# Two windowed transformers on one core: which operand of P times V stays in the array, and where P is divided by its sums

## The chip, the core and the metric

The kernel runs on one core of a Trainium2 chip. Its time is the device time of one execution in microseconds (us); three runs gave a median of 3963.43 us (3961.78 to 3975.84). TensorE is PE in the profile (its weight loads are PEld), VectorE is DVE, ScalarE is ACT, GpSimd is POOL, and SP issues most of the DMAs.

## The reference, cut to what matters

The reference is a chain of four blocks, each a product of an attention and a gated feed-forward net added to x. The change touches two of the feed-forward nets, which are themselves small transformers with attention in a window: "l2" (6 layers, 16 heads, window W = 32, run on 4 sequences of 512 tokens) and "l3" (2 layers, 8 heads, window 64). All is fp32, heads have 64 values. One layer's attention is

```
q = l2norm(q) * qs ; k = l2norm(k) * ksc          # then rotary tables
sim  = einsum('bhwie,bhwje->bhwij', q, k) * 8     # 2W keys for W queries
attn = softmax(where(mask, -max, sim), -1)
out  = einsum('bhwij,bhwje->bhwie', attn, v)
x    = x + out.reshape(b, n, INNER) @ Wo          # then the feed-forward layer
```

A query block of W tokens sees its own block of keys and the one before it, so P (the softmax before the division) has 2W columns for each query and head.

## The kernel before, in words

Both transformers are one class, `_Transformer`. The flag `split` is true for l2 and false for l3. Three generators run interleaved: `queries_keys` (projections, squares, norms, rotary tables, L1268 to L1330), `attention` (L1476 to L1521) and `feed_forward`. Each yields an estimate of the PE time that it has just issued, and `merge` always continues the one that is furthest behind its share; `attention_weight` (L1199) is attention's share. A round of the three is called a slot here: l2 has 48 slots of work (6 layers, 4 sequences, 2 groups of 8 heads), l3 has 8. The order in which an engine then runs its instructions is fixed when the program is built, and it isn't quite the order of the code: in the trace some work stands ahead of work that was written before it.

Attention works in units: 96 in l2 and 32 in l3. A unit is half of a group's heads for 128 T tokens (T = 4 in l2, 2 in l3). In the loop over units, pass i does this:

- `scores` (from L1370) for unit i: a mask goes into two PSUM banks by an identity matmul, then small matmuls (L1389) add the scores, 64 of them in l2 (64 rows by 32 columns of the array each, 64 columns moving) and 16 in l3 (64 by 64, 128 moving). In the middle of them it calls `turn` for unit i-1. After them DVE takes the maxima (L1399), subtracts them (L1403), ACT takes exp (L1408), DVE sums (`rs`, L1410) and inverts the sums (`r`, L1412).
- `turn` (from L1415): 8 PE transposes of P, by `Net.transpose` (L126), and one ACT copy to SBUF (`PT`, L1424).
- `turn_back` (from L1465) for unit i-2: PE transposes of `On` (8 in l2, 4 in l3, again L126) and two ACT copies into `OT` (L1474). After the second unit of a pair come four matmuls of `OT` with `Wo` (by `Net.mm`, L122) and the addition to y (L1513).
- `weigh` (from L1427) for unit i-1: P times V. The turned P is the weight that is loaded, and V moves: 64 matmuls in l2, each 64 rows by 32 columns with 64 columns of V moving, and 16 in l3, each 128 rows by 64 columns with 64 moving. DVE then multiplies by r on the way out of PSUM into `On` (L1454 in l2, L1459 in l3).
- `values` for a later unit: V by matmuls, an ACT copy (L1352) and DMAs.

Each fp32 matmul of the code stands twice in the trace as a weight load and a MATMUL: the 6,144 small matmuls of `weigh` in l2 are 12,288 MATMULs. Transposes stand once.

All PSUM tiles of a transformer come from one pool of four tiles of two banks (`S2`, `M`). On POOL, `queries_keys` puts the sum of two squares (L1294) and the rotary addition (L1298); SP carries the DMAs of Q, K, V and the weights. `part` (L1222 to L1238) loads a weight when it is first asked for; `Wo` has three buffers.

Of the kernel before, what the change touches and what calls it, by code (L numbers as in the profile page):

```python
# [16 lines left out]
F32 = mybir.dt.float32  # L17
# [1153 lines left out]
class _Transformer:  # L1171
    def __init__(self, net, pre, heads, window, pools, consts):
        self.net, self.nc, self.a, self.pre = net, net.nc, net.a, pre
        self.heads, self.W, self.inner = heads, window, heads * 64
        self.GP = heads // 8
        self.NB = 128 // window
        self.split = self.NB == 4
        self.PS, C, self.TB, self.WT, self.QK, self.VP, self.PP, self.TP = pools
        nc, a = self.nc, self.a
        self.T = 4 if self.split else 2  # L1180
        self.NU = self.T * 64 // window
        self.cols = net.load(C, a[pre + "cols"], name=pre + "_cols")
        k = net.load(C, a[consts][:, 0:256], name=pre + "_k", queue=nc.scalar)
        self.ones, self.cen = k[:, 0:128], k[:, 128:256]
        self.tiny = C.tile([128, 1], F32, name=pre + "_tiny")
        nc.vector.memset(self.tiny, 1e-36)
        n = NT // self.T
        self.mask = C.tile([128, n, 512], BF16, name=pre + "_mask")
        nc.gpsimd.dma_start(self.mask, a[consts][:, 256 : 256 + 512 * n].rearrange("p (t n) -> p t n", t=n))
        self.identb = C.tile([128, 128], BF16, name=pre + "_identb")  # L1190
        nc.vector.tensor_copy(self.identb, net.ident)

        self.ve = [C.tile([128, self.NU, 1024 // self.NB], F32, name=f"{pre}_ve{i}") for i in range(2)]
        for i in range(2 if self.split else 1):
            for lo, hi in self.second():
                nc.gpsimd.memset(self.ve[i][lo:hi, 0, :], 0.0)
        self.made, self.shift, self.weights = {}, {}, {}

        self.attention_weight = 20.4 if self.split else 25.0  # L1199
        self.feed_forward_weights = (7.7, 1.7) if self.GP == 2 else (9.4,)  # L1200


        self.lag = 1 if self.split else 0
        self.y = net.xn
# [17 lines left out]
    def part(self, kind, l, gp):  # L1222

        key = kind, l, gp
        if key not in self.weights:
            nc, a, pre = self.nc, self.a, self.pre
            if kind == "qk":
                t = self.WT.tile([128, 1024], F32, name=pre + "_wqk", bufs=2)
                nc.sync.dma_start(t, a[pre + "Wqkv"][l][:, 1024 * gp : 1024 * (gp + 1)])
            elif kind == "v":  # L1230
                t = self.WT.tile([128, 512], F32, name=pre + "_wv", bufs=2)
                c = 2 * self.inner + 512 * gp
                nc.sync.dma_start(t, a[pre + "Wqkv"][l][:, c : c + 512])
            else:
                t = self.WT.tile([128, 4, 128], F32, name=pre + "_wo", bufs=3)
                nc.sync.dma_start(t, a[pre + "Wo"][l][512 * gp : 512 * (gp + 1)].rearrange("(t p) n -> p t n", p=128))
            self.weights[key] = t
        return self.weights[key]  # L1238

# [130 lines left out]
    def scores(self, qk, tp, j, last):  # L1370
# [39 lines left out]
        nc.vector.tensor_reduce(rs, P.rearrange("p t g e k -> p (t g e) k"), axis=AX.X, op=ALU.add)  # L1410
        r = net.stat(n, "r")
        nc.vector.reciprocal(r, rs)  # L1412
        return P, r

    def turn(self, u):  # L1415

# [7 lines left out]
        self.nc.scalar.copy(u["PT"], t)  # L1424
        yield 0.9

    def weigh(self, u):  # L1427

        net, nc, W, T = self.net, self.nc, self.W, self.T
        PT, r, vo, ve, tp, j = (u[k] for k in ("PT", "r", "vo", "ve", "tp", "j"))  # L1430
        On = self.PP.tile([128, 2 * T, 2, 64], F32, name=self.pre + "_On", bufs=1)
        o = self.S2() if self.split else self.M()
        for i in range(2 * T):
            g = i % 2
            for bl in range(self.NB):
                c = self.NB * (T * tp + i // 2) + bl
                v, k = (vo if c % 2 else ve), c // 2 - tp * self.NU
                for e in range(2):
                    if self.split:
                        rows, d = slice(64 * e, 64 * e + 64), 64 * (2 * g + j)  # L1440
                        net.mm(
                            o[W * bl : W * bl + W, e, 64 * i : 64 * i + 64], PT[rows, i, W * bl : W * bl + W],
                            v[rows, k, d : d + 64],
                        )
                    else:
                        n, d = 2 * i + e, 64 * (4 * g + 2 * j + e)
                        net.mm(
                            o[W * bl : W * bl + W, 64 * n : 64 * n + 64], PT[:, n, W * bl : W * bl + W], v[:, k, d : d + 64]
                        )
            yield 0.3 if self.split else 0.15  # L1450
        rv = r.rearrange("p (n e) -> p n e", e=2)
        if self.split:
            for e in range(2):
                nc.vector.tensor_tensor(  # L1454
                    On[:, :, e, :], o[:, e, :].rearrange("p (n d) -> p n d", d=64),
                    rv[:, :, e].unsqueeze(2).to_broadcast([128, 2 * T, 64]), ALU.mult,
                )
        else:
            nc.vector.tensor_tensor(  # L1459
                On.rearrange("p n e d -> p (n e) d"), o.rearrange("p (n d) -> p n d", d=64),  # L1460
                r.unsqueeze(2).to_broadcast([128, 4 * T, 64]), ALU.mult,
            )
        u["On"] = On

    def turn_back(self, u, OT):  # L1465

        net, T = self.net, self.T
        t = (self.S2() if self.split else self.M().unsqueeze(1)).rearrange("p a (b q) -> p (a b) q", q=128)
        for i in range(2 * T):
            net.transpose(t[:, i, :], u["On"][:, i].rearrange("p e d -> p (e d)"))  # L1470
        ov = OT.rearrange("p (g j) (t q) -> p j g t q", j=2, t=T)
        tv = t.rearrange("p (t g) q -> p g t q", g=2)
        for g in range(2):
            self.nc.scalar.copy(ov[:, u["j"], g], tv[:, g])  # L1474

    def attention(self, rows):  # L1476

        net, nc, T = self.net, self.nc, self.T  # L1480
        n = NT // T
        units = [dict(l=l, b=b, gp=gp, tp=tp, j=j) for l, b in rows for gp in range(self.GP) for tp in range(n) for j in range(2)]
        of_slot = len(units) // len(rows) // self.GP
        for piece in self.values(units[0]):
            if piece:
                yield piece
        for i in range(len(units) + 2):
            if i > self.lag and i % of_slot == self.lag or i == 1 and self.lag:
                yield None
            u = units[i] if i < len(units) else None  # L1490
            last = units[i - 1] if 0 < i <= len(units) else None
            older = units[i - 2] if i > 1 else None
            if u:
                if i % of_slot == 0:
                    qk = self.made.pop((u["l"], u["b"], u["gp"]))
                if u["j"] == 1:
                    u["ve"], u["vo"] = last["ve"], last["vo"]
                u["P"], u["r"] = yield from self.scores(qk, u["tp"], u["j"], last)
            elif last:
                yield from self.turn(last)  # L1500
            if older:
                if older["j"] == 0:
                    OT = self.TP.tile([128, 4, 128 * T], F32, name=self.pre + "_OT", bufs=1)
                self.turn_back(older, OT)
                yield 0.9 if self.split else 0.45
                if older["j"] == 1:
                    wo = self.part("o", older["l"], older["gp"])
                    p = self.M()[:, 0 : 128 * T]
                    for t in range(4):
                        net.mm(p, wo[:, t, :], OT[:, t, :], t == 0, t == 3)  # L1510
                        yield 0.86 if self.split else 0.43
                    ys = net.tok(self.y, older["b"])[:, 128 * T * older["tp"] : 128 * T * (older["tp"] + 1)]
                    nc.vector.tensor_tensor(ys, ys, p, ALU.add)  # L1513
                older.clear()
            if last:
                yield from self.weigh(last)
            if u and i + 2 < len(units) and u["j"] == 0:
                ahead = self.values(units[i + 2])
                yield from until_none(ahead)
            elif u and i + 1 < len(units):  # L1520
                yield from until_none(ahead)  # L1521
# [185 lines left out]
```

## Time and profile before

| what | value |
|---|---|
| median of 3 runs | 3963.43 us |
| the profiled execution's own time | 3955.01 us |
| its span (first to last instruction) | 3953.3 us |
| PE busy, whole span | 3577.5 us (90%) |
| DVE busy | 2452.6 us (62%) |
| ACT busy | 1845.0 us (47%) |
| POOL busy | 1157.9 us (29%) |
| l2, about 1650 to 3395 us of the span | 48 slots, 37.6 us each in the middle of a layer |
| l3, about 3540 to 3930 us | 8 slots, 51.85 us each in the middle |

The page of a profile gives busy shares over the whole span. Since the program is a row of different stages, the views for one stretch of time (windows, timeline, waits) are the ones to go by for a change that touches only two stages. A busy PE is a PE with some matmul in flight, so the spacing of the starts says more about its speed than the duration of one row.

### The profile page before, as it was taken

What the parts mean: (1) busy time and instruction counts of PE and PEld (TensorE: products, weight loads), DVE (VectorE), ACT (ScalarE), POOL (GpSimd) and SP (SyncE); (2) the same over time, 40 slices, a digit from 0 to 9 for tenths busy, and PEclk for the clock granted to TensorE, in tenths of its full rate; (3) what the DMA queues carried; (4) which work ended last, traced back from release to release, by engine and by line L of the source; (5) the groups of instructions that cost most, each with busy time, mean ns of one, the idle gap of its engine ahead of it and who ended that gap; (6) DMA issues with size and microseconds to landing.
All of it is one profiled execution on the core that took longest, in us unless ns stands there. A gap on an engine that the chain in (4) does not pass through costs nothing.

```text
span 3953.3 us, 105287 instructions
## 1 busy us (share of the span) xinstructions
PE 3577.5 (90%) x46763; PEld 1880.3 (48%) x46891; DVE 2452.6 (62%) x3429; ACT 1845.0 (47%) x2510; POOL 1157.9 (29%) x994
## 2 busy tenths in 40 slices
PE   7786999899999998889999999999999999778887
PEld 4553455444444443444444554554444445445554
DVE  6674555413353341677777787777777777457774
ACT  3343666523133324454555554555455455535555
POOL 1000444300021112533334343343443343033220
PEclk7677999999699999999999999999999999889998
DMA  1000000001000001434344434334334333413221
GB/s 38 8 26 28 1 1 1 30 0 51 2 1 3 3 1 37 106 86 115 88 96 110 98 91 109 95 91 119 93 83 117 86 80 94 130 37 83 54 56 42
DMA packets 123574, 236.12 MB, mean 60 GB/s; under 512 B 29624, under 2 KB 44128, under 8 KB 117728
## 3 DMA queue, kind: packets, MB, share of 16 engines
q1 hardware_dynamic: 114064, 209.58, 21.7%
q10 hardware_dynamic: 8624, 19.29, 1.5%
q8 instruction: 369, 6.05, 0.6%
q0 software_dynamic: 432, 0.51, 0.1%
q14 instruction: 85, 0.70, 0.1%
HBM read 50.08 MB, written 5.54 MB: 14 GB/s over the span
## 4 chain that ended last, share of the span: by engine, by line
PE 62%; DVE 13%; ACT 12%; issue 6%; DMA 3%; POOL 2%; SPq 1%; DVEq 0%; ACTq 0%; POOLq 0%
PE S L122 39%; PE S L126 5%; PE M L122 5%; PE S L1389 4%; PE o L1094 3%; ACT l_P L581 3%; PE o L614 2%; DVE l_rot L1295 2%; DVE rotp L1297 1%; DMA l_tab<-in_k_rot_l 1%; DVE l_rot L1321 1%; PE S L1008 1%; ACT sqp L1293 1%; ACT l_PT L1424 1%; SPq L1328 1%
## 5 line engine op out<-in xcount | busy, mean ns | idle before, releaser
L1298 POOL TENSOR_TENSOR l_rot<-l_rot,rotp 128x1024 f32<-128x1024 f32 x224 | 528.6, 2362 | 324.7 <-DVE rotp L1297 313.3
L1294 POOL TENSOR_TENSOR sqp<-sqp 128x512 f32<-128x512 f32 x224 | 291.5, 1301 | 956.6 <-ACT sqp L1293 952.0
L122 PE MATMUL S<-hb,l_wqk 128*128 128x512 f32 x896 | 476.8, 622 | 38.1 <-ACT l_PT L1424 10.7
L1293 ACT ACTIVATE sqp<-S 128x1024 f32<-128x1024 f32 x224 | 230.2, 1027 | 305.1 <-PE S L122 304.1
L1321 DVE SCALAR_TENSOR_TENSOR l_rot<-S,l_rot 128x1024 f32<-128x1024 f32 x224 | 264.6, 1219 | 133.8 <-ACT S L1318 110.6
L126 PE MATMUL S<-core,l_P 128*128 128x128 f32 x1856 | 266.9, 288 | 40.1 <-ACT l_P L1408 17.3
L122 PE MATMUL S<-l_KT,l_QT 32*128 32x256 f32 (+7 forms) x1536 | 264.2, 510 | 34.7 <-ACT l_P L1116 14.5
L1295 DVE TENSOR_TENSOR l_rot<-S,l_tab 128x1024 f32<-128x1024 f32 x224 | 271.2, 1211 | 24.6 <-ACT sqp L1293 24.0
L1389 PEld LDWEIGHTS S<-l_qk 64*32 64x32 f32 (+1 forms) x13312 | 178.5, 108 | 217.7 <-issue 211.2
L1116 ACT ACTIVATE l_P<-S 128x1024 f32<-128x1024 f32 x160 | 156.7, 1022 | 252.3 <-PE S L122 251.7
L126 PEld LDWEIGHTS S<-core,l_P 128*128 128x128 f32 x1856 | 213.3, 146 | 128.1 <-issue 39.3
L1297 DVE TENSOR_TENSOR rotp<-S,l_tab 128x1024 f32<-128x1024 f32 x224 | 270.8, 1209 | 1.4 <-POOL l_rot L1298 1.3
L1389 PE MATMUL S<-l_qk 64*32 64x64 f32 (+1 forms) x13312 | 249.5, 230 | 18.8 <-DMA l_qk<-l_rot 1.7
L122 PE MATMUL S<-sqp,l_k 128*128 128x512 f32 x448 | 251.9, 648 | 13.4 <-POOL sqp L1294 6.6
L122 PE MATMUL S<-l_wv,hb 128*64 128x256 f32 (+1 forms) x1600 | 237.2, 400 | 5.5 <-DVE rotp L1297 4.2
L1069 DVE TENSOR_REDUCE l_mx<-S 128x2 f32<-128x768 f32 (+1 forms) x192 | 155.0, 864 | 136.7 <-PE S L1008 136.7
L122 PEld LDWEIGHTS S<-l_ve,l_PT 64*32 64x32 f32 (+1 forms) x6656 | 164.3, 108 | 152.5 <-issue 124.9
L1399 DVE TENSOR_REDUCE mx<-S 128x16 f32<-128x1024 f32 (+1 forms) x128 | 156.3, 1221 | 116.1 <-PE S L1389 112.2
L122 PEld LDWEIGHTS S<-hb,l_wqk 128*128 128x128 f32 x896 | 147.2, 191 | 168.6 <-issue 92.0
L122 PE MATMUL S<-l_OT,l_wo 128*128 128x512 f32 (+1 forms) x512 | 218.9, 543 | 8.3 <-DVE ffu L1551 7.9
L1120 POOL TENSOR_SCALAR_AFFINE_SELECT l_P<-l_P 128x256 f32<-128x256 f32 x256 | 99.4, 406 | 417.0 <-ACT l_P L1116 411.6
L1317 ACT ACTIVATE S<-S,l_tiny 128x1024 f32<-128x1024 f32 x112 | 121.9, 1089 | 198.4 <-PE S L122 180.2
(358 smaller groups left out, 6580.1 us busy)
## 6 DMA issues: line engine op xcount, KB each, us to landing
l_qk<-l_rot SPq DMA_DIRECT2D x896, 128.0 KB
l_ve<-l_vo SPq DMA_DIRECT2D x112, 256.0 KB
l_ve<-l_vo SPq DMA_DIRECT2D x96, 224.0 KB
l_tab<-in_k_rot_l ACTq DMA_DIRECT2D x16, 1024.0 KB
l_wqk<-in_l2Wqkv SPq DMA_DIRECT2D x12, 512.0 KB
l_wv<-in_l2Wqkv SPq DMA_DIRECT2D x12, 256.0 KB
l_wo<-in_l2Wo SPq DMA_DIRECT2D x12, 256.0 KB
l_ve<-l_vo SPq DMA_DIRECT2D x24, 128.0 KB
```

The lines of the kernel that those rows point to most:

```text
L122: self.nc.tensor.matmul(out, lhsT, rhs, start=start, stop=stop)
L126: self.nc.tensor.transpose(out, in_, self.ident[:n, :n])
L1069: nc.vector.tensor_reduce(mxv[:, bs, 2 * m + e, 3 - i], s[u][:, :, c : c + n], axis=AX.X, op=ALU.max)
L1116: nc.scalar.activation(P[u], s[u], AF.Exp, scale=scale)
L1293: nc.scalar.activation(sq, p, AF.Square)
L1294: nc.gpsimd.tensor_tensor(sq[:, 0, :], sq[:, 0, :], sq[:, 1, :], ALU.add)
L1295: nc.vector.tensor_tensor(t[:, g], p, tab[:, 0], ALU.mult)
L1297: nc.vector.tensor_tensor(m, p, tab[:, 1], ALU.mult)
L1298: nc.gpsimd.tensor_tensor(t[:, g], t[:, g], m[:, ::-1, :], ALU.add)
L1321: nc.vector.scalar_tensor_tensor(t[:, g], p[:, g, :].unsqueeze(1).to_broadcast([128, 2, S]), 1e12, t[:, g], ALU.min, ALU.mult)
L1389: net.nc.tensor.matmul(sv[W * bl : W * bl + W, e, t, g, :].rearrange("p (s k) -> p s k", s=2), qk[0][r, g, j, W * c : W * c + W], kw, star ...
L1399: nc.vector.tensor_reduce(mx, flat, axis=AX.X, op=ALU.max)
```

## The change

- In `weigh` the two operands change places: 64 columns of V are the weight that is loaded, and the turned P moves (32 columns in l2, 64 in l3). O comes out with its 64 values on partitions and tokens along the free axis, as `Wo` needs it, so ACT copies it straight into `OT`; `turn_back` with its transposes is gone, and so is `On`.
- In l2 the matmuls alternate over four quadrants of 64 by 64 of the array: head e reads rows 64e, and the block's parity s sends it to columns 64 (e xor s) and to PSUM bank s. Heads stand the other way round for odd blocks, so `Wo` is kept twice, the second time with its halves exchanged (two more DMAs for each load, two buffers instead of three), and the four `Wo` matmuls of 512 columns become eight of 256.
- r can no longer be multiplied onto O, whose queries are along the free axis now. P is divided by its sums before it is turned: one POOL multiplication of 128 by 1024 for each unit, in place.
- In l3 the shape of the `weigh` matmuls stays (128 rows by 64 columns, 64 moving).

```diff
-        self.attention_weight = 20.4 if self.split else 25.0
+        self.attention_weight = 18.6 if self.split else 23.0
...
-                t = self.WT.tile([128, 4, 128], F32, name=pre + "_wo", bufs=3)
-                nc.sync.dma_start(t, a[pre + "Wo"][l][512 * gp : 512 * (gp + 1)].rearrange("(t p) n -> p t n", p=128))
+                t = self.WT.tile([128, 2 if self.split else 1, 4, 128], F32, name=pre + "_wo", bufs=2)
+                wo = a[pre + "Wo"][l][512 * gp : 512 * (gp + 1)].rearrange("(t p) n -> p t n", p=128)
+                nc.sync.dma_start(t[:, 0], wo)
+                if self.split:
+                    nc.sync.dma_start(t[0:64, 1], wo[64:128])
+                    nc.sync.dma_start(t[64:128, 1], wo[0:64])
...
-        return P, r
+        Pn = P.rearrange("p t g e k -> p (t g e) k")
+        nc.gpsimd.tensor_tensor(Pn, Pn, r.unsqueeze(2).to_broadcast([128, n, 2 * W]), ALU.mult)
+        return P
...
-                        rows, d = slice(64 * e, 64 * e + 64), 64 * (2 * g + j)
-                        net.mm(
-                            o[W * bl : W * bl + W, e, 64 * i : 64 * i + 64], PT[rows, i, W * bl : W * bl + W],
-                            v[rows, k, d : d + 64],
-                        )
+                        rows, d, s = slice(64 * e, 64 * e + 64), 64 * (2 * g + j), bl % 2
+                        x = 64 * (e ^ s)
+                        net.mm(ov[x : x + 64, s, i, bl // 2, :], v[rows, k, d : d + 64], PT[rows, i, W * bl : W * bl + W])
...
-    def turn_back(self, u, OT):
...
-        for i in range(2 * T):
-            net.transpose(t[:, i, :], u["On"][:, i].rearrange("p e d -> p (e d)"))
...
+        for s in range(2 if self.split else 1):
+            n = 2 * W
+            src = (o[:, s, :] if self.split else o).rearrange("p (t g q) -> p g t q", g=2, q=n)
+            dst = OT[:, s].rearrange("p (g j) (t q) -> p j g t q", j=2, q=n)
+            nc.scalar.copy(dst[:, j], src)
...
-                    for t in range(4):
-                        net.mm(p, wo[:, t, :], OT[:, t, :], t == 0, t == 3)
-                        yield 0.86 if self.split else 0.43
+                    parities = 2 if self.split else 1
+                    pv = p.rearrange("p (x s q) -> p s x q", s=parities, q=W)
+                    for s in range(parities):
+                        for t in range(4):
+                            net.mm(pv[:, s], wo[:, s, t, :], OT[:, s, t, :].rearrange("p (x q) -> p x q", q=W), t == 0, t == 3)
+                            yield 0.43
```

## The prediction

> **What bounds the kernel now.** I read the page first, then the windows of the two transformers, then groups by form, then the timeline of one unit in each, last the waits of PE. From the page, the share of the engines in the chain that ended last; from the windows view, l2 (without its ends) and l3:
>
> ```profile
> PE 62%; DVE 13%; ACT 12%; issue 6%; DMA 3%; POOL 2%; SPq 1%; DVEq 0%; ACTq 0%; POOLq 0%
> ```
> ```profile
> 1687.00:3340.00 1653.00, 1578.73 (x27055) 815.83 (x27142) 1283.61 (x1415) 842.81 (x958) 644.61 (x394) 1.00 0.40 96
> 3540.00:3933.00 393.00, 346.17 (x2819) 198.65 (x2846) 272.45 (x348) 218.91 (x272) 99.41 (x68) 0.97 0.25 59
> ```
>
> Columns: stretch, length, busy time (and count) of PE, PEld, DVE, ACT, POOL, granted clock, DMA. In l2 PE is busy 95.5% of the time at full clock, DVE 78%, POOL 39%: PE's work sets the end, and a microsecond of it taken away is worth about a microsecond. In l3 PE is busy 88%, so waits count there too.
>
> The timeline of PE shows what the pieces take. In l2, one unit's P times V (128 MATMULs between the first two lines) and one `turn_back`; in l3, scores on four quadrants, a `turn_back` and P times V:
>
> ```profile
> 2201.36 0.25 PE L122 MATMUL S<-l_ve,l_PT 64*32 64x64 f32 x2
> ...
> 2202.78 0.65 PE L122 MATMUL S<-l_wv,hb 128*64 128x256 f32 x4
> ...
> 2211.40 1.09 PE L126 MATMUL S<-core,l_On 128*128 128x128 f32 x8
> 2212.33 1.02 PE L122 MATMUL S<-hb,l_wqk 128*128 128x512 f32 x2
> ```
> ```profile
> 3730.91 1.09 PE L126 MATMUL S<-core,l_P 128*128 128x128 f32 x8 [0.59 <-ACT l_P L1408]
> ...
> 3737.58 0.27 PE L122 MATMUL S<-l_ve,l_PT 128*64 128x64 f32 x1
> ...
> 3738.56 0.22 PE L122 MATMUL S<-l_vo,l_PT 128*64 128x64 f32 x1
> 3738.71 0.39 PE L122 MATMUL S<-l_mask,l_identb 128*128 128x512 bf16 x1
> 3739.25 0.67 PE L1389 MATMUL S<-l_qk 64*64 64x128 f32 x16
> ```
>
> A row lasts 0.22 us but starts follow each other closely: (2202.78 - 2201.36) less 0.15 us for the change of tile shape (the hole between 3738.56 and 3738.71) is 1.27 us for 128, so **9.9 ns for each MATMUL in l2's weigh**. In l3's weigh it is 0.98 us for 31 steps, 31.6 ns, on two tiles of 128 by 64. In l3's scores (0.67 - 0.27) / 15 = 26.7 ns on four tiles of 64 by 64. Two more views, groups by form and waits of PE in l2:
>
> ```profile
> L595 POOL TENSOR_TENSOR l_P<-l_P,l_r 128x1024 f32<-128x1024 f32 x48 | 90.8, 1893 | 68.3 <-DVE l_r L586 58.4 <-PE S L126 9.9
> ```
> ```profile
> PE S L122 <- DVE l_On L1454: 18.3, 16, 1.4
> PE S L122 <- ACT l_PT L1424: 14.3, 33, 0.8
> PE S L122 <- DVE rotp L1297: 10.3, 11, 2.0
> PE S L122 <- ACT l_OT L1474: 9.2, 24, 1.3
> ```
>
> **The change, part by part.**
>
> *turn_back goes.* In l2 8 transposes from 2211.40 to 2212.33, 0.93 us, in 96 units: -89. In l3 4 of them take (0.66 - 0.27) / 3 x 4 = 0.52 us (row 3742.37, 0.66 us), in 32 units: -17. Both are on PE, the bound.
>
> *weigh in l2.* As many loads and MATMULs, but a load brings 64 columns instead of 32, and 32 columns move instead of 64, on four tiles instead of eight. No row has this shape with so short a stream. From below: 128 columns are loaded and moved every 0.93/8 = 116 ns in the transposes, so 64 columns need about 58 ns, on four tiles 14.5 ns; at best 13.6, if the last transposes' 109 ns is the true step. From above: the four-quadrant row itself, 26.7 ns, though its 128 moving columns account for all of it. The nearest row is l3's weigh: the load is the same 64 columns, 31.6 ns on two tiles, thus 15.8 on four. I take 14.5: with 32 columns moving, only the load is left to wait for. Cost 12,288 x (14.5 - 9.9) ns = +57; ends +45 and +206.
>
> The Trainium skill, "TensorE: Matmul & The Clock Gate", section "Wait — 56ns, not 53.3ns?", says that start to start never drops below about 25 ns, however few columns move. That speaks against the change, for fewer moving columns would then buy nothing; by it this term would be +186 and the whole sum +91, but the 9.9 ns above already break the rule, and the measurement decides.
>
> *weigh in l3* keeps its shape: 0.
>
> *Wo.* Eight matmuls of 256 columns for four of 512: l3's rows of 256 columns start 216 ns apart (3736.19 to 3737.58, six and a change of shape), those of 512 in l2 429: 0. Two more DMAs for each of 12 loads, some 0.45 us each on SP, ahead of K and Q transfers that PE needs a slot later; the slot hides them. With two buffers a load waits for the last use of the layer before; such waits of SP exist now (10.0 us is the longest) and cost PE nothing. I take 0; if five changes of layer each passed 10 us on, +50.
>
> *DVE's product goes*, 2 x 0.67 us a unit in l2. DVE isn't the bound, so only PE's waits for it are worth something: 18.3 us above. ACT's two copies now free that PSUM tile, at 0.59 us each, and the third PSUM tile of a unit isn't taken at all. I take -15; ends 0 and -28 (both waits).
>
> *P is divided on POOL.* A unit's op is L595's: 1.9 us (L1298, which reads two full tiles, takes 2.36). The turning of P waited for exp until now; it will wait for the sums (1.22 us), r (0.24) and POOL. In l2 that is covered: the median from the end of r to the P transposes is 9.1 us, a tenth of the units have under 4. What stands behind the op on POOL matters more: sums of squares (L1294), for which PE's ones-matmul waits. Pairing them by time, 47 of 192 in l2 have less than 1.9 us to spare, 60 us short in all if each met a division. There is one division for two of them: 30 at most. POOL is idle 61% of the time and the order can use that: +10. In l3 the second window has no such slack. P transposes start at 3730.91, 0.05 us after exp; with r at 3732.34, POOL in L1298 until 3733.38 and 1.9 us, P is ready at 3735.3, 4.4 us later. PE has 0.59 us of scores, a hole of 1.40 and 0.96 of a projection to fill in: 1.45 left. The first unit of a slot (transposes at 3697.51, r at 3698.46) is 2.9 us late, with 2.4 us of other work: 0.5 left. The other two have 2.3 and 7.2 us from r. 8 slots x 1.95 = +16; ends 0 and 8 x 7.3 = +58, if PE fills nothing.
>
> The Trainium skill, "GPSIMD Engine Reference", section "Engine selection", advises elementwise work on VectorE, POOL being about half as fast with two inputs. Here DVE's product of 128 by 1024 takes 1.21 us against POOL's 1.89, so on DVE P would be ready 0.7 us sooner, at most some 10 us over l3's slots (sum -48), for 116 us more in l2 on an engine that is busy 78%.
>
> **The sum**: -89 - 17 + 57 + 0 - 15 + 10 + 16 = -38 on the profiled execution's 3955.0 us, which lies 8.4 us under the median; taken off the median, 3963.4 - 38 = **3925**.
>
> **Rivals.**
>
> 1. *More is won*: the loads run at 13.6 ns, both PSUM waits go, the order covers P's lateness: -89 - 17 + 45 - 28 = -89, 3874. For it: the median slack of 9.1 us in l2.
>
> 2. *Slower: weigh's load of 64 columns is the new bound of PE.* Place: the 12,288 MATMULs of l2's P times V. At the four-quadrant row's 26.7 ns the sum is -89 - 17 + 206 - 15 + 10 + 16 = +111, 4074. Without this term the sum is -95, which 7.7 ns on each MATMUL uses up: from 17.6 ns on, the kernel is slower. Against it: in that row four loads start within 13 ns of each other, so quadrants load side by side. For it: nothing shows more than one load every 26 ns on such quadrants.
>
> 3. *The wait for P takes the place of turn_back*: l3's 58 and POOL's 30 in full, +24, 3987. For it: PE already stands waiting for exp in l3.
>
> 4. *PE's work wasn't on the path*, or what goes is given back by another wait in the slot: 3963. Against it: 95.5% busy, 62% of the chain.
>
> **Numbers.** Forecast 0.40 (own range 3885 to 3965: 0.34 faster, 0.06 the same), rival 1 0.14, rival 2 0.18, rival 3 0.18 (0.06 the same, 0.12 slower), rival 4 0.10. Measurement tells about 0.5% from no change, so faster means under 3943.6 and slower over 3983.2: faster 0.34 + 0.14 = 0.48, same 0.06 + 0.06 + 0.10 = 0.22, slower 0.18 + 0.12 = 0.30. The range, 3865 to 4005, leaves out rival 2 and the edges.
>
> **What would show it.** Right: no rows of L126 on `On`; l2's weigh rows 64*64 with 128 starts in about 1.9 us; POOL busy about 250 us more; l2's slots at 37.6 - 2 x 0.35 us or less; P transposes of l3 waiting for POOL in two units of four. Wrong: starts over 17.6 ns apart; PE waiting for L1294 or for the division in l2; l3 slots over 54 us; SP held by the loads of `Wo`.

## The result, and the profile after

The changed kernel takes **4077.95 us** (median of 4 runs) against 3965.61 us of the kernel before (median of 4): a ratio of 1.0289, 95% interval 1.0262 to 1.0316. It is slower by 112 us where the forecast was 38 us faster. The profiled execution took 4075.76 us, with a span of 4074.0 us.

First the two stretches that the prediction looked at, in the windows view of the changed kernel (stretch, length, busy time and count of PE, PEld, DVE, ACT, POOL, granted clock, DMA):

```profile
1690.00:3440.00 1750.00, 1603.80 (x27451) 896.72 (x27452) 1192.54 (x1264) 863.63 (x980) 820.32 (x488) 0.97 0.39 95
3640.00:4040.00 400.00, 312.84 (x2563) 182.57 (x2560) 246.91 (x295) 185.21 (x208) 146.55 (x93) 0.90 0.24 56
```

In l2 PE is busy 91.6% (95.5% before) at a clock of 0.97 (1.00), in l3 78% (88%) at 0.90 (0.97). POOL's share of l2 has risen from 39% to 47%. PE has less to do and the kernel takes longer, so the loss is in waits and in the clock. The output additions (the last step of a unit pair) give the stages' lengths: from the first to the last of l2's 48 it was 1737.2 us, now 1802.2 (+65); of l3's 16 it was 361.5, now 399.7 (+38); the stretch between has grown from 146.8 to 163.7 (+17). The chain of waits is no help here: followed back from the end it breaks off inside l3, and the line says so by its small shares.

```profile
PE 6%; DVE 2%; ACT 1%; POOL 1%; issue 1%; DMA 0%; POOLq 0%; ACTq 0%; DVEq 0%
```

What PE waits for does help. Five lines of l2 (1690 to 3440 us), the first line of l3 (3640 to 4040 us), and the first line of l3 in the kernel before (3560 to 3900 us); the columns are the total in us, how often, and the longest:

```profile
PE S L122 <- DMA l_wqk<-in_l2Wqkv: 50.7, 5, 15.3
PE S L122 <- DVE rotp L1302: 35.6, 40, 3.6
PE S L122 <- ACT l_PT L1431: 18.7, 52, 0.8
PE S L122 <- DMA l_wv<-in_l2Wqkv: 6.8, 2, 3.9
...
PE S L122 <- POOL l_P L1419: 4.8, 4, 1.2
```
```profile
PE S L126 <- POOL l_P L1419: 66.4, 17, 8.1
```
```profile
PE S L126 <- ACT l_P L1408: 12.1, 8, 5.4
```

Two things are new and large: in l2 PE waits for the **weights of Q and K** at each change of layer, 7.6 to 15.3 us at a time, and in l3 the transposes of P wait for the **divided P**, 66 us, where they waited 12 us for exp. The waits for `On` are gone, as forecast; the wait for `rotp` (a PSUM tile of K or Q that VectorE still has to read) has grown from 10 to 36 us.

The steps of the change themselves took the time that was worked out for them. In the timeline of PE, one unit's P times V of 128 MATMULs starts at 2239.83 us and the next work at 2241.82:

```profile
2239.30 0.59 PE L122 MATMUL S<-hb,l_wqk 128*128 128x512 f32 x1
2239.83 0.25 PE L122 MATMUL S<-l_PT,l_ve 64*64 64x32 f32 x2
...
2241.82 0.65 PE L122 MATMUL S<-l_wv,hb 128*64 128x256 f32 x4
```

(1.99 - 0.15) / 128 = 14.4 ns for each MATMUL, on four tiles of 64 by 64, against the 14.5 that were taken; 0.15 us is again the change of tile shape. GpSimd's group of the division:

```profile
L1419 POOL TENSOR_TENSOR l_P<-l_P,r 128x1024 f32<-128x1024 f32 x128 | 244.6, 1911 | 164.4 <-DVE r L1417 142.8
```

### The profile page after: what moved, and what is told of

The parts are those of the page before. It is cut to its first block, busy times and chain, and to the rows that moved or that the text cites. A ratio compares the mean times of both kernels' runs of the same rounds, so it can differ in the third digit from the quotient of the medians.

```text
span 4074.0 us, 104444 instructions
## 1 busy us (share of the span) xinstructions
PE 3578.9 (88%) x46379; PEld 1951.9 (48%) x46379; DVE 2322.2 (57%) x3205; ACT 1834.2 (45%) x2468; POOL 1396.5 (34%) x1122
## 5 line engine op out<-in xcount | busy, mean ns | idle before, releaser
L122 PE MATMUL S<-hb,l_wqk 128*128 128x512 f32 x896 | 488.5, 645 | 108.5 <-DMA l_wqk<-in_l2Wqkv 50.7
L1300 DVE TENSOR_TENSOR l_rot<-S,l_tab 128x1024 f32<-128x1024 f32 x224 | 271.3, 1211 | 101.8 <-ACT sqp L1298 99.7
L1419 POOL TENSOR_TENSOR l_P<-l_P,r 128x1024 f32<-128x1024 f32 x128 | 244.6, 1911 | 164.4 <-DVE r L1417 142.8
L122 PE MATMUL S<-l_KT,l_QT 32*128 32x256 f32 (+7 forms) x1536 | 266.9, 515 | 34.6 <-ACT l_P L1116 14.5
L122 PEld LDWEIGHTS S<-l_PT,l_ve 64*64 64x64 f32 (+1 forms) x6656 | 223.7, 138 | 117.9 <-issue 74.0
L1302 DVE TENSOR_TENSOR rotp<-S,l_tab 128x1024 f32<-128x1024 f32 x224 | 270.3, 1207 | 0.0
L122 PE MATMUL S<-l_PT,l_ve 64*64 64x32 f32 (+1 forms) x6656 | 248.9, 223 | 20.4 <-ACT l_PT L1431 12.5
L122 PE MATMUL S<-l_PT,l_vo 64*64 64x32 f32 (+1 forms) x6656 | 247.5, 223 | 2.3 <-issue 2.2
L1464 ACT COPY l_OT<-S 128x512 f32<-128x512 f32 x224 | 124.0, 586 | 247.7 <-PE S L122 247.5
```

The source lines that it names most:

```text
L122: self.nc.tensor.matmul(out, lhsT, rhs, start=start, stop=stop)
L1300: nc.vector.tensor_tensor(t[:, g], p, tab[:, 0], ALU.mult)
L1302: nc.vector.tensor_tensor(m, p, tab[:, 1], ALU.mult)
L1419: nc.gpsimd.tensor_tensor(Pn, Pn, r.unsqueeze(2).to_broadcast([128, n, 2 * W]), ALU.mult)
L1464: nc.scalar.copy(dst[:, j], src)
```

## The experiments

In each, the time above the kernel before is the difference of its median from the median of the runs of before made with it. The changed kernel's is +112. The ratios are the record's and can differ from the quotient of the medians by up to 0.001. "Slots" are the distances of l2's output additions.

**Theories.** A: in l2, the load of the next layer's Q and K weights stands too late in SP's queue. B: in l3, P's way to the transposes has become longer than the work that PE can do meanwhile. Rivals: P times V is the new bound, or POOL's queue is, or the clock falls for its own reasons.

### e1_wqk_early: the load one slot earlier

SP's own rows show theory A. The last slot of a layer in the changed kernel:

```profile
1838.65 18.07 SPq L1333 DMA_DIRECT2D l_qk<-l_rot  x16
1856.77 0.58 SPq L1229 DMA_DIRECT2D l_wqk<-in_l2Wqkv  x1
1857.46 0.39 SPq L1233 DMA_DIRECT2D l_wv<-in_l2Wqkv  x1
```
```profile
1843.75 1.95 PE L122 MATMUL S<-l_wv,hb 128*64 128x256 f32 x16
1860.96 2.04 PE L122 MATMUL S<-hb,l_wqk 128*128 128x512 f32 x2 [15.26 <-DMA l_wqk<-in_l2Wqkv]
```

The load is issued at 1856.77 behind 16 transfers of K and Q, which wait one after the other for VectorE's products; PE has stood since 1845.70. The other four waits, 7.6 to 10.2 us each (not three of 15, as the expectation below has it), are for a layer's second such load (the other group of heads), which stands behind 8 transfers. In the kernel before, the first load stood ahead of the last slot's transfers:

```profile
1810.57 2.53 SPq L1328 DMA_DIRECT2D l_qk<-l_rot  x4
1813.19 0.53 SPq L1229 DMA_DIRECT2D l_wqk<-in_l2Wqkv  x1
...
1832.77 20.70 SPq L1328 DMA_DIRECT2D l_qk<-l_rot  x16
```

The edit:

```
     self.made[l, b, gp] = made
+    if b == B - 1 and (l + 1, 0) in rows:
+        self.part("qk", l + 1, gp)
     yield None
```

> The changed kernel, but the Q and K weights of l2's next layer are asked for one slot earlier, so that SP issues that load ahead of the K and Q transfers of two more groups. Nothing else is changed. Theory A (the order of SP's queue): three waits of PE for DMA l_wqk of 15 us each, 50.7 us in all, came from that load standing behind transfers that themselves wait; they go, l2's slots at a change of layer come back from 50 us to 38, and the time is 4078 - 45 to 4078 - 60, about 4025. l3 stays as it is (36 + 22 us for two slots). Rival (PE's own work in l2's P times V, or its lower granted clock, makes up the 65 us, and the wait only collects it): less than 15 us is won, another wait of PE stands in the same slots.

Measured: 4025.36 us, +65, ratio 1.0167 (1.0149 to 1.0185). The wait for `l_wqk` is gone from the list, l2's slots at a change of layer are back from 50 us to 39 to 41, and l2 takes 1744.4 us. 48 us are theory A's. l3 is as it was (399.7 us).

### c1_before_early: the same edit on the kernel before

> The kernel before with the same earlier request for l2's next Q and K weights as in e1_wqk_early, as a control. There the load stood ahead of the transfers already, so that it should win little: 3950 to 3965. Were 20 us or more won, the earlier request would be a gain of its own, and e1 would say less of the change.

Measured: 3965.68 us, +3, ratio 1.0009 (0.9996 to 1.0022). The early request is no gain of its own.

### e2_l3_old: l3 without the change

```
-    self.attention_weight = 18.6 if self.split else 23.0
+    self.attention_weight = 18.6 if self.split else 25.0
...
+    if self.split:
         nc.gpsimd.tensor_tensor(Pn, Pn, r..., ALU.mult)
...
+    if not self.split:
+        self.turn_back(older, OT)
```

> The changed kernel, but only l2 has the change: l3 keeps P in the array, divides O on VectorE and turns it back, as before. Theory B (l3's P waits for its sums, r and POOL): PE's wait of 66.4 us for the division in l3 goes, the wait for exp of about 12 us and 17 us of transposes come back, l3's two slots are again 52 us instead of 58: 4078 - 38 = 4040, some 10 less if the stretch between l2 and l3 comes back too. Rival (l3 is longer because its clock is lower or because Wo has two buffers): l3's slots stay at 56 us or more, time 4065 to 4078.

Measured: 4043.1 us, +82, ratio 1.0207 (1.0188 to 1.0226). l3 is back at 361.4 us and the stretch between l2 and l3 at 151.2. So some 12 of the 17 us between the stages belong to l3's new start-up, not to l2. In all, 30 us are gone, fewer than the 38 in l3 and these 12.

### e3_both: l2 changed with the load in time, l3 old

> Both of the above: l2 has the change with its next Q and K weights asked for one slot earlier, l3 is the old one. If theories A and B hold and their gains add: 4078 - 52 - 38 = 3988, or 3975 with the stretch between l2 and l3. Were l2's gain the one that was forecast (-89 + 57 - 15 + 10 = -37), it would be 3965.6 - 37 = 3929. Rival (l2's new P times V is no gain, for the clock or the waits take it back): 3965 or above.

Measured: 3971.86 us, +11, ratio 1.0030 (1.0018 to 1.0043). A and B together explain 101 of the 112 us. They don't simply add: alone A is worth 48 us (e1) and B 30 (e2), after the other A is worth 71 (e2 to e3) and B 53 (e1 to e3). And the rest is not the -37 that the terms give for l2: l2 takes 1742 us against 1737. From start to start of PE's instructions, less the idle time that the trace gives before each, PE's own work from the first to the last of l2's output additions is 1641.5 us in e3 against 1668.5 before (92 us less of transposes, 49 more of P times V, 13 more of the products for Q and K); PE's waits there are 100.6 us against 68.7. So PE's work fell by 27 us, near the forecast, and its waits took that back. Which waits, and why, is the second half of this study.

### e14_l3_nodiv: what the division costs l3

The kernel of e1 that leaves out l3's division of P by its sums:

```
+    if self.split:
         nc.gpsimd.tensor_tensor(Pn, Pn, r..., ALU.mult)
```

> The run e1_wqk_early (4025; l2 and l3 have the change), but l3 doesn't divide P by its sums: it leaves out that division in l3, so the output is not the reference's. The transposes of P then wait for exp alone. If l3's 38 us and the stretch ahead of it come from P's lateness as such, they go, and l3's transposes, 17 us, are won besides: two slots of 50 us, 4025 - 38 - 17 - 18 = 3952. If it is GpSimd's work or the lower clock, 4000 or above.

Measured: 3964.45 us, +4, ratio 1.0000 (0.9981 to 1.0020), 61 us less than e1. l3 takes 351.3 us, 10 less than before the change: without the division the change wins 10 of the 17 us that the transposes were to give there, and the division costs 48 in l3 and more ahead of it. The longest wait of the changed kernel shows why it is so much more than the 1.9 us of the operation. PE, VectorE, ScalarE and GpSimd from 3707 to 3719 us:

```profile
3708.05 1.10 PE L1394 MATMUL S<-l_qk 64*64 64x128 f32 x32
3717.28 1.97 PE L126 MATMUL S<-core,l_P 128*128 128x128 f32 x8 [8.13 <-POOL l_P L1419]
```
```profile
3712.70 1.22 DVE L1415 TENSOR_REDUCE rs<-l_P 128x8 f32<-128x1024 f32 x1
3713.84 1.21 DVE L1404 TENSOR_REDUCE mx<-S 128x8 f32<-128x1024 f32 x1
3714.97 0.19 DVE L1417 RECIPROCAL r<-rs 128x8 f32<-128x8 f32 x1
```
```profile
3710.32 1.28 ACT L1271 ACT_TABLE_LOAD   x1
3711.61 1.06 ACT L1413 ACTIVATE l_P<-l_P 128x1024 f32<-128x1024 f32 x1
```
```profile
3715.33 1.90 POOL L1419 TENSOR_TENSOR l_P<-l_P,r 128x1024 f32<-128x1024 f32 x1 [7.18 <-DVE r L1417]
```

exp ends at 3712.67, where the old kernel's transposes would have started. Now the sums follow, then r stands behind the next unit's maximum on VectorE (1.2 us), and only then POOL: 4.6 us more, and PE has nothing but these transposes at the head of its queue. The clock is 0.90 in this stage (0.97 before), so work behind such holes is slower as well.

### e4_dve: P divided on VectorE

```
-    nc.gpsimd.tensor_tensor(Pn, Pn, r..., ALU.mult)
+    nc.vector.tensor_tensor(Pn, Pn, r..., ALU.mult)
```

> The changed kernel, but P is divided by its sums on VectorE instead of GpSimd, in l2 and l3 (1.21 us for 128 by 1024 instead of 1.91, and no queue of squares ahead of it). If the wait in l3 is the chain exp, sums, r, division as such, P comes 0.7 us sooner in each of 32 units and not later for GpSimd's other work: 10 to 25 us are won in l3. If GpSimd's queue was most of it (its op on K and Q of 2.4 us stands ahead), 40 us. In l2 VectorE gets 116 us more work and no product of On: waits for rotp and sums of squares that came from GpSimd's division (25 us more than before) go, others for VectorE come; 0 plus or minus 25. Time 4035 to 4085.

Measured: 4144.37 us, +184, ratio 1.0474 (1.0450 to 1.0498): outside all that was expected. l3 still waits 45 us for the divided P. And the product is not 1.21 us long: over l2 (1900 to 3400 us) the group of 74 has a mean of 1722 ns, and the timelines of VectorE and GpSimd show one of 2.35.

```profile
1998.94 2.35 DVE L1419 TENSOR_TENSOR l_P<-l_P,r 128x1024 f32<-128x1024 f32 x1
```
```profile
1997.87 2.35 POOL L1303 TENSOR_TENSOR l_rot<-l_rot,rotp 128x1024 f32<-128x1024 f32 x1 [3.77 <-DVE rotp L1302]
```

GpSimd's addition ends at 2000.22, and VectorE's product 1.07 us after it: the product has waited for it. Products with no GpSimd operation beside them take 1.22 us. The prediction's 1.21 us is that of rows that read one operand from PSUM (L1300 and L1302 take as much here). The run doesn't price the product alone: in l2 PE's waits for `l_wqk` are 70.8 us here (50.7 in the changed kernel), and 42.6 us more have no releaser that the trace shows, so the order has moved as well.

### e8_nodiv and c3_before_div: the division in l2

e8_nodiv is e3_both without l2's division; c3_before_div is the kernel before with it:

```
     nc.vector.reciprocal(r, rs)
+    if self.split:
+        Pn = P.rearrange("p t g e k -> p (t g e) k")
+        nc.gpsimd.tensor_tensor(Pn, Pn, r..., ALU.mult)
...
-    nc.vector.tensor_tensor(On[:, :, e, :], o[:, e, :]..., rv[:, :, e]..., ALU.mult)
+    nc.vector.tensor_copy(On[:, :, e, :], o[:, e, :]...)
```

> The run e3_both (3972) without l2's division of P on GpSimd: it leaves out the division of P by its sums in l2, so the output is not the reference's. It prices that operation. The forecast had it at 10 us, 30 at most: then 3942 to 3962. The 30 us of PE's waits for rotp stay, if they come from VectorE's written order (it stands waiting for exp with the sums of P while a table product that PE waits for is next), and go if they come from GpSimd's queue: then 3935 or less.

> The kernel before, but in l2 P is divided by its sums on GpSimd, and VectorE only copies O out of the PSUM tile where it multiplied it by r (the same two operations of 128 by 512). P times V and turn_back are the old ones; the SP order of the weights' loads is that of before. It prices the step of the division alone, with the lateness of P and all that the order makes of it. The forecast: +10, 30 at most, 3973 to 3993. Rival (the division is free, as e8_nodiv's 11 us may come from the place of its transfers): 3963 within 5. Other rival (P's lateness moves PE's order and costs more): 4000 or above.

Measured: e8 3961.11 us (-1), 12 less than e3; c3 3973.56 us, +13, ratio 1.0027 (1.0012 to 1.0043). Taken away or put in, the division in l2 costs 12 to 13 us, near the forecast's 10. In e8 the wait for `rotp` is what it was in e3, to the tenth:

```profile
PE S L122 <- DVE rotp L1302: 30.4, 38, 1.9
```

So that wait doesn't come from the division in GpSimd's queue. Ten of the 38 have the same 1.90 us, one in every four slots: VectorE's next operation there is the sums of P, which wait for exp, and the table products that would free PE's tile stand behind them.

### e9_two_quadrants: is P times V on the path?

The kernel of e3 with P times V on two quadrants, without the two extra loads of Wo:

```
-    x = 64 * (e ^ s)
+    x = 64 * e
...
-    net.mm(pv[:, s], wo[:, s, t, :], ...)
+    net.mm(pv[:, s], wo[:, 0, t, :], ...)
```

> The run e3_both (3972), but l2's P times V uses only the two quadrants on the diagonal instead of all four, and Wo needs no second copy (two DMAs less for each of 12 loads). If a load of 64 columns is what each MATMUL waits for, as l3's 31 ns on two tiles says, a unit's 128 MATMULs take 3.9 us instead of 1.9: 96 units by 2.0 us, 190 us more, about 4160. Rival (the P times V is hidden by something else that bounds l2's slots, so that its 14.5 ns never mattered): under 4030.

Measured: 4159.62 us, +197, ratio 1.0507 (1.0490 to 1.0524), 186 more than e3. The step over l2 is then 31.4 ns instead of 16.6 with the changes of shape included (29.1 instead of 14.6 within a unit whose 128 MATMULs stand together), which is 178 us more of PE's work, and l2 takes 166 us more. Four quadrants work side by side, and work *added* to PE is paid for nearly in full.

### c2_one_transpose and e17_one_transpose_early: what is PE time worth that is taken away?

The kernel before, but leaving out seven of the eight transposes of each `turn_back` in l2, and the same with the early request of e1:

```
-    for i in range(2 * T):
+    for i in range(1 if self.split else 2 * T):
         net.transpose(t[:, i, :], ...)
+    if self.split:
+        t = t[:, 0:1, :].to_broadcast([128, 2 * T, 128])
```

> The kernel before, but l2's turn_back does one transpose of eight (the two copies read that one eight times): it leaves out seven eighths of the turning back of O in l2, so the output is not the reference's. Everything else, the planner's weights and the copies, is that of before. It prices the first step of the forecast alone: 96 units by 7 x 116 ns = 78 us of PE's time, thus 3963 - 78 = 3885, if a microsecond of PE's work in l2 is worth about one. Rival (the wait behind it is what counts: the built order and the copies keep the slot where it is, as l2's slots with the change did): 3935 to 3963.

> The run c2_one_transpose (4027; the kernel before with one transpose of eight in l2's turn_back, so it leaves out seven eighths of the turning back there) with l2's Q and K weights of the next layer asked for one slot earlier. c2 has 74 us of waits for l_wqk, and its ordinary slots of l2 take 37.4 us against 37.5 before, though PE has 1.6 us less to do in each. If those slots are held by something beside PE (all of PE's new waits there are for a PSUM tile that ACT or VectorE must still read), only the late loads go: 4027 - 74 - some 15 of the clock behind them = 3938, a gain of 20 to 30 where 78 us of PE's work are gone. Rival (PE's time is worth its time, once the loads are in time): 3885 to 3900.

Measured: c2 4026.98 us, **+66**, ratio 1.0161 (1.0127 to 1.0195); e17 3959.26 us, -5, ratio 0.9987 (0.9971 to 1.0003). Taking 78 us of PE's work out of l2, and nothing else in the code, makes the kernel 66 us slower, and with the loads in time it is worth 5 us (the interval runs from 11 us won to 1 lost). c2's first waits of PE, then SP's rows at a change of layer, and PE's:

```profile
PE S L122 <- DMA l_wqk<-in_l2Wqkv: 74.2, 5, 17.7
PE S L122 <- ACT l_PT L1424: 43.4, 49, 1.2
PE S L122 <- DVE l_On L1454: 27.7, 26, 1.7
PE S L122 <- ACT l_OT L1476: 15.2, 41, 2.0
```
```profile
2142.22 15.50 SPq L1328 DMA_DIRECT2D l_qk<-l_rot  x16
2157.76 0.59 SPq L1229 DMA_DIRECT2D l_wqk<-in_l2Wqkv  x1
```
```profile
2162.02 2.05 PE L122 MATMUL S<-hb,l_wqk 128*128 128x512 f32 x2 [13.95 <-DMA l_wqk<-in_l2Wqkv]
```

Two answers stand in these lines. The load of Q and K's weights stands behind 16 transfers again, and PE waits 13.95 us for it: the order of SP's queue is made when the kernel is built, and it moved because the transposes are gone. And an ordinary slot takes 37.4 us against 37.5 before: other waits have taken the place of the transposes. In e17 PE's work in l2, from start to start, is 61 us less than before and its waits are 63 us more. The three lines on PSUM tiles (P^T still being copied, `On`, `OT`) hold 73 us in e17 against 42 before, half of that; most of the matmuls that wait there (of `hb` and `l_wqk`, or the mask) read nothing of what is copied, so it is the tile that they wait for. The other half is spread over `l_wv`, `l_rot` and waits with no releaser that the trace shows.

### e10_order, e11_old_order, e13_old_weights_early, e12_old_order_all: the order made by hand

e10 is e3 that asks for V's weights early too, yields a piece between exp and the sums, and has the attention's share of before; e11 gives e2's l2 the planner's weights of before, with empty pieces; e13 is e11 with e1's edit; e12 is e11 with l3 changed as well.

```
e10: -self.attention_weight = 18.6 if self.split else 25.0
     +self.attention_weight = 20.4 if self.split else 25.0
     ...
      def values(...):
          self.last_vo = vo
     +    if self.split and u["b"] == B - 1 and tp == NT // self.T - 1 and u["l"] + 1 < ...:
     +        self.part("v", u["l"] + 1, u["gp"])
      nc.scalar.activation(Pf, Pf, AF.Exp, scale=8.0)
     +if self.split:
     +    yield 0.9
e11:  if older:
     +    yield 0.9 if self.split else 0.45
     -    yield 0.43
     +    if t % 2: yield 0.86
```

> The run e3_both (3972) with two changes of order in l2 and no change of work: the load of V's weights of the next layer is asked for right after the last use of the old ones, and a piece of 0.9 of the planner's weight is let in between exp and the sums of P, so that VectorE needn't stand waiting for exp ahead of the table products. If the rest of l2's lost gain is such waits (rotp 30 us, l_wv 14 us, and a clock that falls for some 5 us behind each hole of 2 us or more), 25 to 45 us are won: 3927 to 3947, near the forecast 3925 + 17 for l3's transposes that stay. Rival (VectorE or GpSimd, or the clock for its own reasons, bound the slot): within 10 us of 3972.

> The run e2_l3_old (l2 has the change, l3 is the old one), but in l2 the planner is given the weights of before: the attention counts 20.4, a piece of 0.9 is yielded where turn_back stood, with no work in it, and Wo's eight matmuls yield four pieces of 0.86. The work is that of e2_l3_old; only the order in which the other passes' instructions lie between is that of before, so that the weights' loads stand where they stood. If the 65 us in l2 are all order (loads behind transfers, VectorE's written order, the clock behind their holes), the gain that was forecast for l2 appears: -89 + 57 - 15 + 10 = -37, 3926, and the clock in l2 is 1.00 again. Rival (part of it is in the new work itself: its copies, the wait for the sums, the division): 3945 to 3975.

> The run e11_old_order (4047) with l2's Q and K weights of the next layer asked for one slot earlier. In e11 two waits of 14 us for l_wqk are shown, and SP stood 69 us for the buffer of V's weights ahead of it. If the late loads, with the clock behind their holes, are what makes e11 slow, 50 to 70 us are won, as e1 won 53: 3978 to 3997. The planner's weights would then make no difference, and e3's 3972 is what this P times V gives. Rival (VectorE's written order and P's lateness make e11 slow): 4020 or above.

> As e11_old_order, but l3 has the change too, with the planner's weights of before there as well (25.0, and an empty piece of 0.45 where turn_back stood). If l3's wait for the divided P is not a matter of the planner's order but of the distance between scores and transposes, l3's two slots are 57 to 58 us again, and the time is that of e11 + 35 to 45. Rival (the planner's order made l3's wait): e11 - 17 to e11 + 16.

Measured: e10 4011.24 us (+49), e11 4047.5 (+83), e13 4014.78 (+54), e12 4107.41 (+142). **All four missed what was expected of them.** In e10 the wait for `l_wv` is gone, but `l_wo` has taken its place (16.9 us) and `rotp` stays at 26.5. In e11 two waits for the Q and K load stay, 28.1 us; both loads stand behind transfers of K and Q once more. With the early request, e13 still is 43 above e3: waits for `rotp` of 39.6 us, for `l_vo` 12.0, for `l_rot` 19.7. It seems that the order that is built follows the operations' dependences, too, so that the planner's old pieces don't bring the old order back; that is not shown, and these runs don't price the order. One thing e12 does show: l3's two slots are 58 to 60 us there as well, and the time is 60 us above e11's, so B is no matter of the planner's pieces.

### e15_pairs and c4_before_pairs: holding PSUM tiles for less long

The waits for PSUM tiles suggest that the four tiles hold the slots. One of them can be followed in the trace, the tile of K or Q: four MATMULs of `hb` and `l_wqk` fill it and `rotp` is its last reader. In l2 before it is held 11.0 us in the middle, four times in a slot of 37.5 us, so 1.2 of the four tiles on average; other work lies between its two products. Let both products be one piece, in l2 and l3:

```
     for h in range(2):
         net.mm(o..., w[:, c : c + 128], hk if i else hb)
-        yield 0.86
+    yield 1.72
```

> The run e3_both (3972; l2 has the change with the load in time, l3 is the old one), but the two products of 512 columns that fill one PSUM tile of K or Q are one piece for the planner (1.72) instead of two of 0.86, in l2 and l3: no other work lies between them. The tile is then held for less long (it is 10 us now, from the first product to the second table product), and there are four tiles. If PSUM tiles hold l2's slots at 37.5 us beside PE, slots go down to 36.6 to 37.1, 20 to 45 us less: 3927 to 3952. Rival (another bound, or the moved order costs as much): 3960 to 4000.

> The kernel before with the same pieces of 1.72 as e15_pairs, as its control. Before, PE is busy 95.5% of l2 and waits 66 us there, half of it for PSUM tiles: at most 30 us can be won, 3935 to 3963. If e15 wins no more than this run, the gain is none of the change's.

Measured: e15 3951.8 us, -12, ratio **0.9971** (0.9956 to 0.9987), 20 less than e3's median and at the edge of what was expected; c4 3965.12 us, +1, ratio 1.0004 (0.9992 to 1.0017). A tile of K or Q is held 8.4 us in e15 (10.1 in e3) and 8.3 in c4. l2 takes 1729 us in e15, 13 less than in e3. The edit is worth nothing to the kernel before and some 20 us to the new P times V. But the gain is not one of waits: in l2 PE waits 105 us in e15 (101 in e3), its three lines on tiles (`rotp`, P^T, `OT`) fall by only 3 us, and it is the work from start to start that falls by 18, since the products of K and Q now follow each other at 463 ns instead of 497. In c4 these products won 21 us too (450 ns instead of 479), and PE's waits grew by 22. So the time for which the tiles are held is not shown to be the cause. e15 is the one version here that beats both kernels, by 0.3%, and only l2 of the change is in it.

## Why the prediction was wrong

**Size and sign.** The sum was -38 and the result +112. The 150 us between them fall into three nearly equal parts: l2's own terms (-37 forecast, +11 in e3), late loads that had no term (48, e1) and l3 (-1 forecast, +53 from e1 to e3). The prediction's own steps:

- *turn_back goes, -89 in l2.* **This is the step that failed**: "a microsecond of it taken away is worth about a microsecond". c2 and e17 took 78 us away; it cost 66 us, and with the loads in time it won 5. PE, busy 95.5%, has just 66 us of waits in l2, but waits grew by as much as the work fell, 63 us for 61 in e17 and 22 for 23 in c4: something else is nearly as late. Half of e17's new waits are for the copies that free a PSUM tile. e9 shows the other side, added work is paid for almost in full. Here the busy share told what more work would cost, not what less work would win. In l3, 10 of the 17 us arrived (e14).
- *weigh in l2, +57.* The duration was right (14.4 ns against 14.5), and rival 2, whose 4074 us lies near the result, is wrong in its mechanism: at the full clock starts were 14.4 ns apart, not 26.7. As with the first term, the two together were worth not -32 but about nothing: PE's work fell by 27 us from before to e3, and its waits grew by 32.
- *Wo, 0, or 50 if five changes of layer each passed 10 us on.* The place and the price were near (five waits, 50.7 us), the transfer was another one: PE didn't wait for Wo's loads, but for Q and K's weights, which stood behind 8 or 16 transfers. The prediction read SP's queue as it was before and took its order for given. SP did stand 75.2 us for Wo's buffers (42.0 before, 33.7 in e1), a sign that the prediction had named; no run changes the buffers alone, so what that cost stays open. e1 prices the late loads at 48 us, c2 shows that the missing transposes alone bring such waits.
- *PSUM waits, -15.* The wait for `On` went as forecast, `OT`'s fell to 6 us; `rotp` rose by 25. Sum: above zero.
- *POOL's division in l2, +10.* Right: 12 to 13 (e8, c3).
- *l3, P late, +16, ends 0 and 58.* The mechanism was right, the size was off: 48 us inside l3 (e14 against e1), 61 over the whole with the start-up, against the 16 that were taken: near the upper end of 58 inside l3, beyond it over the whole. The term counted on PE's other work to fill the wait; in the built order the transposes stand at the head of PE's queue with nothing ahead of them, and r stands behind the next unit's maximum.
- *The clock* had no term. What it costs in l2 (PE's busy time times one less the granted clock, summed over stretches of 2 us from 1690 to 3400 us) is by this estimate 3 us before, 25 after, 19 in e1 and 18 in e3. So some 15 us of what e3 lacks are the clock behind its holes, mostly those where PE waits for `l_wv` and `rotp`; e15, which is faster, has 21.

**The account.** Late loads with their clock 48, l3 with its start-up 53 (e1 to e3), what l2 keeps 11: 112. Taken in the other order it is 30 for l3 (e2) and 71 for the loads. Rival 4 (PE's work wasn't on the path) holds for l2, rival 3 (the wait for P takes the place of turn_back) for l3; the prediction gave each a part and let neither decide.

What stays open: what holds l2's slots beside PE. The tiles still being copied are one candidate: they are half of e17's new waits, but holding one of them for less long didn't shorten the waits. VectorE's written order (30 us of `rotp` in e3, 33 in e15) is a second, and no run here took that wait away.

## What to carry to other kernels

Before PE work is priced at its own length, look for what stands ready to wait in its place: a tile that is copied right behind it, a queue whose order the build makes anew. Then split a run's time into PE's work and PE's waits: a gain that shows in one and is missing in the sum stands in the other. Where order is made at build time, a change is first an edit of every queue: find in the profile after which load has moved, and ask for it earlier, before the change itself is judged. A value that gains two more steps (sums, division) on its way to an engine with an order of its own must have that much work queued ahead of it in that order; an idle share or work that lies further back does not cover it.

## What the runs showed of the hardware

**The clock halves behind a short hole.** e3_both, windows around a hole of PE of 3.0 us (2191.65 is the last start before it):

```profile
2188.00:2192.00 4.00, 4.00 (x132) 2.57 (x132) 4.00 (x6) 0.75 (x2) 2.90 (x2) 1.00 0.72 169
2194.00:2196.00 2.00, 0.76 (x4) 0.59 (x6) 1.46 (x3) 1.46 (x2) 0.84 (x1) 0.58 0.22 84
2198.00:2200.00 2.00, 2.00 (x8) 0.72 (x5) 0.00 (x0) 1.01 (x1) 0.00 (x0) 0.50 0.37 84
2202.00:2204.00 2.00, 2.00 (x55) 1.15 (x55) 0.00 (x0) 0.60 (x1) 0.00 (x0) 1.00 0.89 204
```

The granted clock is 0.50 to 0.71 for some 6 us after it, with PE busy: by estimate, the hole costs about as much again. Of the three other holes of 3.0 to 3.6 us in l2, two did the same and one did it for some 3.4 us. Of ten holes of 1.90 us, four did it, for some 3.4 us, and six did not. The record of the clock explains that: it has steps of 3.41 us at 1.00 or 0.50. In e3's l2 the nine steps at full clock in which PE was busy less than 45% were each followed by a step at 0.50, and none of the other 480 was; a hole of 1.90 us that lies across two steps leaves both above that. In the changed kernel, e1 and e15 steps between 42% and 57% went either way. The Trainium skill, "TensorE: Matmul & The Clock Gate", section "HAM oscillation — how this bites in real kernels", asks for no idle gaps of PE over about 3.4 us. The half clock agrees; the threshold here is lower, and the measurement decides.

**VectorE and GpSimd shut each other out.** In e4_dve a product of VectorE with both operands in SBUF took 1.22 us alone and ended 1.1 us after GpSimd's operation where one was running. GpSimd's addition takes 3.3 us instead of 2.36 where such a product had begun first. The Trainium skill, "SBUF — State Buffer", section "SBUF: two separate sides", says it: a VectorE operation with two SBUF inputs and a GpSimd operation that reads SBUF hold a shared port in turn, for the whole instruction. The runs agree, and the prediction, which weighed VectorE for the division at 1.21 us, had not looked there.

**Four quadrants work side by side.** MATMULs with 64 columns of weights come at 14.6 ns each on four tiles of 64 by 64 (e3), and at 29.1 ns on two (e9).
